# A graph layer on one core: each gather of source rows takes 127 rows instead of 128

## The chip, the cores and the metric

The kernel runs on one core of one Trainium2 chip. The core has a matrix engine (PE), a vector engine (DVE), an activation engine (ACT), GpSimd (POOL) and a queue engine for transfers (SP); sixteen DMA engines move data between the core's memory (SBUF) and the device's (DRAM). The metric is the device time of one execution in microseconds (us), and lower is better. The change is judged by the median of several executions.

## The reference: what is computed

A graph has 12,500 nodes with 96 numbers each and 412,500 edges, sorted by the node that they point to (`dst`). Per edge, a message is made from the row of its source node, the row of its target node and four numbers of its own; the messages are normalized over all edges, summed by target, and added to a term of the node itself.

```python
node_feat = _mlp(x, W_node, b_node, g_node, beta_node)
edge_feat = _mlp(edge_attr, W_edge, b_edge, g_edge, beta_edge)
row, col = (edge_index[0], edge_index[1])
message = jnp.concatenate([x[row], x[col], edge_feat], axis=1)
message = _mlp(message, W_msg, b_msg, g_msg, beta_msg)
agg = jax.ops.segment_sum(message, col, num_segments=node_feat.shape[0])
return agg + node_feat
...
x = _layernorm(x + _L0_gnn_ref(...))
```

`_mlp` is `relu(h @ W + b)`, normalized by mean and variance over all rows. So the sums of the messages and of their squares over all 412,500 edges are needed, as well as the sums by target.

## The kernel before

**Tables.** Since the message's matrix acts on three concatenated parts, the part of the source is done once per node: `p_tab` holds x times the first 96 rows of the matrix, `q_tab` x times the second 96. Per edge, a row of `p_tab` is fetched by its source, and what `q_tab` and the edge's own numbers give is added.

**Edges in blocks.** A *tile* is 128 edges, one on each partition. Four tiles are a group (`GT`), four groups of 512 edges are a block (`BG`, 16 tiles, 2048 edges). The sorted edges are laid out so that a tile takes 32 edges from each of the block's four groups: partitions 0 to 31 from the first, 96 to 127 from the fourth. There are 3223 tiles, 806 groups and 202 blocks, the last of them with seven tiles.

**The gather (L205 to L218).** POOL fetches the source rows: one indirect transfer per tile, with 128 row numbers from one column of `src`, writes 128 rows of 384 bytes to `pg`, one on each partition. 3220 tiles are fetched so (64 of them from x itself for the first four blocks, whose product with the matrix is done later, 3156 from `p_tab`); the last tile of three groups (`EARLY`) is fetched row by row by SP. The tile `pg` holds two groups, and seven such tiles are a ring of 14 groups. Each gather signals one of eight counters in turn, and waits for the gather eight before it, which used the same one.

**Ahead of the main loop.** From the start POOL gathers the rows of 29 blocks, which SP stores to DRAM as they come (`spill`, L237), and after them fills the ring with 14 groups. Meanwhile the tables are made, the edges' numbers are split into parts of bf16 and stored as `stack_d`, the node term is computed, and `edge_norm` (L394) computes the statistics of the edge features: per block three matmuls (L413), a relu on ACT (L417) and three statistics on DVE (L419), on tiles `eas` that DVE sets to ones first (L401).

**The main loop (L731 to L767)** walks over the blocks in an order fixed by `plan`: from block 29 on, with the 29 stored blocks strewn in between (they are read back as `pb`, and so need no gather then). Each step `k` is one group. For the block two steps of blocks ahead PE makes the edge features and the window of places (L605/L614) and ACT applies relu (L621, 127 partitions: 96 features, 31 window places; `rhs` holds the matching rows, which SP loads per block from 31 rows of `q_tab` at L578). For the next block PE makes `z` (L626) and DVE transposes it in 32x32 squares so that edges stand on partitions (L636). For the present group pair `message` (L649) adds the gathered rows to `z` and cuts at zero, on DVE. ACT squares the message (L663), DVE adds the squares up (L674). DVE writes a 0/1 matrix of the edges' targets within the block's window (L655), PE multiplies the messages by it (L693), and DVE adds the sums to `agg` (L712, L713). At the end of a step `ahead_of` puts one more group of gathers on POOL (L763): the first group of a pair may only overwrite its `pg` when `message` has read it.

The instructions of PE, DVE, ACT, POOL and SP in the main loop stand in the order in which the code is written (`manual_schedule`); elsewhere a scheduler orders PE, DVE and ACT.

**The end (L770 to L798)** handles the last, incomplete block of two groups: POOL folds the squares (`collect`, L682 and L684), PE adds the sums over partitions, and then the output is normalized and written (from L975 on).

Of the kernel before, what the change touches and what calls it, by code (L numbers as in the profile page):

```python
# [13 lines left out]
F32 = mybir.dt.float32  # L14
# [3 lines left out]
AF = mybir.ActivationFunctionType  # L18
OP = mybir.AluOpType
AX = mybir.AxisListType  # L20
# [4 lines left out]
N, C, E, ED = 12500, 96, 412500, 4  # L25
EPS = 1e-5
P = 128
# [13 lines left out]
RW = 7  # L41
NBQ = RW * 32
# [27 lines left out]
NW = WS * (BG - 1) + WN + 1  # L70
QE = 32
BT = BG * GT
LT = NT - (NBL - 1) * BT
LE, LS = LT * QE, 7
CL, CE = 3, 1
# [35 lines left out]
def gnn(ctx, tc, t):  # L111
# [93 lines left out]
    def gather(g, pg, without=0):  # L205
        c, o = g * GT // CW, g * GT % CW
        tab, idx = (t["x"], src_raw[:, g * GT:]) if g < RAW * BG else (p_tab, src[:, c % 2, o:])
        if c and o == CW // 2 and (c + 1) * CW < NTP:
            sources(c + 1)
        made = [nc.gpsimd.indirect_dma_start(  # L210
            out=pg[:, i, :], out_offset=None, in_=tab[:, :],
            in_offset=bass.IndirectOffsetOnAxis(ap=idx[:, i:i + 1], axis=0)).ins
            for i in range(min(GT, NT - g * GT) - without)]
        for x in made[:-1]:
            tc.add_to_no_dep_group(f"rows{g}", x)
        if made[:-1]:
            tc.declare_fence(made[-1], group=f"rows{g}")
        return pg  # L218

    def blocks():  # L220

        waiting = []
        for b in range(SPILL // BG + BEHIND):
            if b < SPILL // BG:
                for i in range(0, BG, 2):
                    pg = ring.tile([P, 2, GT, C], F32, name="pg")
# [167 lines left out]
    def edge_norm():  # L394

        with tc.tile_pool(name="es", bufs=2) as work, tc.tile_pool(name="es1", bufs=1) as one, \
# [3 lines left out]
            for x in eas:  # L400
                nc.vector.memset(x[C:], 1.0)  # L401
            for b in range(NBL):
                if b % J == 0:
                    yield
                    ea, n = eas[b // J % 2], min(J, NBL - b)
                    stacked(ea[:, :n, :], b, n)
                    if b + n == NBL:
                        nc.sync.dma_start(ea[ON:, n - 1, :], t["one"])
                for i in range(NS):
                    k = NS * b + i  # L410
                    if k % 2 == 0:
                        pr = ps.tile([P, 2, GE], F32, name="pr")
                    nc.tensor.matmul(pr[:, k % 2, :], wide[:, P * i:P * (i + 1)], ea[:, b % J, :],  # L413
                                     start=True, stop=True)
                    if k % 2:
                        r = work.tile([P, 2, GE], F32, name="r", bufs=4)
                        nc.scalar.activation(r, pr, AF.Relu)  # L417
                        for o in (1, 0):
                            nc.vector.bn_stats(stats[:, (k - o) % NS, (k - o) // NS, :], r[:, 1 - o, :])  # L419
# [66 lines left out]
    def fast(ring):  # L486
        y0s, got = [], {}

        def ahead_of(g):
            if g % 2 == 0:  # L490
                got[g] = ring.tile([P, 2, GT, C], F32, name="pg")
            if g < NG:
                gather(g, got[g // 2 * 2][:, g % 2, :, :])
# [27 lines left out]
        with tc.tile_pool(name="fix", bufs=1) as fix, tc.tile_pool(name="msg", bufs=2) as work, \  # L521
# [117 lines left out]
            def message(k, m=2, n=2 * GT):  # L639

                s, g = steps[k]
                o = k % 2 * GT
                z = zs[s % 2][:, g % BG * GT:g % BG * GT + n, :]
                h = hb[k // 2 % HP].rearrange("p m t c -> p (m t) c")[:, o:o + n, :C]
                if order[s] < RAW:
                    nc.vector.tensor_scalar(h, z, 0.0, MOST, op0=OP.max, op1=OP.min)
                    return
                rows = got[g // 2 * 2].rearrange("p m t c -> p (m t) c")[:, o:o + n, :]
                nc.vector._custom_dve(TENSOR_ADD_SAT, out=h, in0=z, in1=rows, s0=MOST, s1=0.0)  # L649
# [11 lines left out]
            def squared(k, m=2, n=GT):  # L661
                sq = work.tile([P, 2, GT, C], F32, name="sq")
                nc.scalar.activation(sq[:, :m, :n, :], hb[k // 2 % HP][:, k % 2:k % 2 + m, :n, :C], AF.Square)  # L663
                return sq

            def valid(t):

                left_over = E - (NBL - 1) * BT * P - (BG - 1) * LE
                return P - QE + min(max(left_over - (t - (NBL - 1) * BT) * QE, 0), QE) if t >= (NBL - 1) * BT else P

            def moments(sq, at_last):

                sq = sq.rearrange("p m t c -> p (m t) c")
                nc.vector.tensor_tensor(wide_sq, wide_sq, sq, op=OP.add)  # L674
                if at_last:
                    nc.vector.tensor_reduce(squares, wide_sq.rearrange("p t c -> p c t"), axis=AX.X, op=OP.add)

            def collect(x, n):
                plus = nc.gpsimd.tensor_add
                while n > 1:  # L680
                    half = n // 2
                    plus(x[:, :half * C], x[:, :half * C], x[:, (n - half) * C:n * C])  # L682
                    n -= half
                plus(squares, x[:, :C], squares)  # L684

# [32 lines left out]
            with tc.manual_schedule(engines={ET.SP, ET.Pool, ET.PE, ET.DVE, ET.Activation}):  # L718
# [12 lines left out]
                for k in range(last):  # L731
# [24 lines left out]
                    if s + 2 < len(order):  # L756
# [13 lines left out]
                s, g = len(order) - 1, steps[last][1]  # L770
                m = NT - (g + 1) * GT
# [7 lines left out]
                sq.append(work.tile([P, 2, GT, C], F32, name="sq"))  # L779
                nc.vector.memset(sq[1][:, 0, :, :], 0.0)  # L780
                h = hb[(n - 1) // 2 % HP]
                for t in range(m):
                    r = valid((g + 1) * GT + t)
                    nc.scalar.activation(sq[1][:r, 0, t, :], h[:r, 1, t, :C], AF.Square)
                collect(sq[0][:, 0, :, :].rearrange("p t c -> p (t c)"), GT)
                sums(last)
                at_end = place(s - 1), place(s)
                unread(1)
                collect(sq[1][:, 0, :, :].rearrange("p t c -> p (t c)"), m)
                add(s - 1, at_end[0])  # L790
                sums(n - 1)
                unread(1)
                square_sum = by_place[s % 2][:C, P:P + 1]
                nc.tensor.matmul(square_sum, squares, ones, start=True, stop=True)
                unread(BUSY)
# [11 lines left out]
    def general():  # L807

        with tc.tile_pool(name="gd", bufs=1, space=DRAM) as gd, tc.tile_pool(name="gfix", bufs=1) as fix, \
# [111 lines left out]
            with tc.For_i(0, NI, 1) as it:  # L921
# [3 lines left out]
                for g in range(-AHEAD, IG):  # L925
                    if g + AHEAD < IG:
                        got[g + AHEAD] = gather(si, di, (g + AHEAD) * GT, GT, P)
                    if g < 0:
# [3 lines left out]
                    nc.vector.memset(ea, 1.0)  # L932
                    nc.sync.dma_start(ea[:ED], t["ea"][i::BG, bass.ds(it * (IG // BG) + g // BG, 1), :]
                                      .rearrange("k b e -> k (b e)"))
# [6 lines left out]
            for j, (t0, nt, rows) in enumerate(REST):  # L941
# [6 lines left out]
                nc.vector.memset(ea, 1.0)  # L948
                of = t["ea"][i::BG, g // BG, o:o + nt * rows] if g < BG * (NBL - 1) else t["ea_end"][i::BG, o:o + nt * rows]
                nc.sync.dma_start(ea[:ED, :nt * rows], of)  # L950
                message(j, got, ea[:, :nt * rows], df, sp, c, nt, rows, stats[:, NI * IG + j, :])
# [135 lines left out]
```

## Time and profile before

| what | value |
|---|---|
| median of 3 runs (lowest to highest) | 4238.63 us (4232.95 to 4239.72) |
| the profiled execution: time, span of its trace | 4239.95 us, 4238.2 us |
| gathers from `p_tab` on POOL | 3156, median 947 ns |
| first and last start of them | 83.6 and 4175.2 us |
| DVE's wait for a gather at L649 | 583.0 us, 172 times |
| DMA engines' mean share in the main loop | 0.24 |

How to read it: a profile of one execution gives the busy time of each engine, groups of instructions by line with their count, busy time and mean duration, and for the idle time ahead of an instruction what ended it ("<-DMA pg" is a transfer into pg that landed, "<-issue" is that nothing the profile shows was waited for). In a tile's view the three durations are the least, the median and the greatest in ns. DMA views give packets, megabytes and rates; their rows of 40 digits or numbers are 40 equal slices of a stretch, the digits in tenths of the sixteen engines' time.

### The profile page before, as it was taken

To read this page: it belongs to the slowest core of one execution; us is meant where nothing else is said; L and a number is where in the kernel's file an instruction comes from. 1 tells how busy PE (TensorE), PEld (TensorE's weight loads), DVE (VectorE), ACT (ScalarE), POOL (GpSimd) and SP (SyncE) were. 2 spreads that over 40 slices of the span, in tenths; PEclk is the share of its full clock that TensorE was granted. 3 is DMA by queue.
4 is the path that set the end of the run, shared out by engine and by line. 5 is a ranking of instruction groups with operands and counts; after the bars stand their busy time and mean duration, and the time that the engine had idled before them with its cause. 6 is when DMAs were issued, how large, how long until landed. Compare 5 with 4: busy or idle time off the path is not lost.

```text
span 4238.2 us, 34504 instructions
## 1 busy us (share of the span) xinstructions
PE 2500.7 (59%) x10245; PEld 1391.0 (33%) x10245; DVE 3340.1 (79%) x4652; ACT 1117.9 (26%) x1229; POOL 3180.5 (75%) x3248
## 2 busy tenths in 40 slices
PE   4156664776655655666655565555655556666556
PEld 3041111433333332333333333333333333333335
DVE  2469998998887877878878887787878877878775
ACT  1438882222221211212112211111112112211111
POOL 7777776777777777777777777777777777777775
PEclk7557776888877787877777877787788787777776
DMA  8746562222222223222222222222222222222222
GB/s 229 267 139 149 134 148 51 57 57 64 50 56 53 57 71 78 63 56 56 55 56 50 57 54 55 57 57 54 56 57 53 50 63 50 54 57 55 56 44 64
DMA packets 215122, 316.63 MB, mean 75 GB/s; under 512 B 126785, under 2 KB 133275, under 8 KB 212095
## 3 DMA queue, kind: packets, MB, share of 16 engines
q0 software_dynamic: 103040, 158.48, 17.6%
q1 hardware_dynamic: 98923, 150.92, 12.1%
q10 hardware_dynamic: 12960, 4.93, 0.5%
q8 instruction: 82, 1.34, 0.1%
q14 instruction: 117, 0.96, 0.1%
HBM read 258.19 MB, written 55.89 MB: 74 GB/s over the span
## 4 chain that ended last, share of the span: by engine, by line
POOL 37%; DVE 25%; issue 19%; DMA 12%; PE 6%; ACT 1%; SPq 0%; DVEq 0%; POOLq 0%; ACTq 0%
POOL pg L210 37%; DMA pg<-p_tab,src 9%; DVE big L636 9%; DVE estats L419 8%; DVE h L649 3%; DVE mixed L674 2%; PE z L626 1%; PE pa L693 1%; PE py L981 1%; DVE at L655 1%; DMA q_tab<-trow 1%; PE py L383 1%; PE pt L194 0%; DMA x<-in_ea 0%; DVE part L424 0%
## 5 line engine op out<-in xcount | busy, mean ns | idle before, releaser
L210 POOL DMA_INDIRECT pg<-p_tab,src x3156 | 3097.6, 981 | 995.2 <-issue 899.6
L636 DVE STREAM_TRANSPOSE big<-z 32x512 f32<-32x512 f32 x2424 | 1715.3, 708 | 90.8 <-PE z L626 29.6
L693 PE MATMUL pa<-at,h 128*97 128x80 f32 x6446 | 934.1, 304 | 1346.3 <-DVE h L649 1327.5
L693 PEld LDWEIGHTS pa<-at,h 128*97 128x97 f32 x6446 | 881.7, 217 | 1818.7 <-DVE h L649 1677.1
L626 PE MATMUL z<-left,rhs 128*96 128x512 f32 (+1 forms) x1616 | 1079.7, 757 | 2.1 <-DVE big L636 2.1
L663 ACT ACTIVATE sq<-h 128x768 f32<-128x768 f32 x403 | 339.5, 842 | 2750.2 <-DVE h L649 2710.1
L649 DVE CUSTOM_DVE_ANT_0 h<-big,pg 128x768 f32<-128x768 f32 x346 | 325.3, 940 | 585.1 <-DMA pg<-p_tab,src 583.0
L621 ACT ACTIVATE left<-pr 127x1024 f32<-127x1024 f32 x404 | 405.6, 1004 | 18.1 <-PE pr L614 18.1
L674 DVE TENSOR_TENSOR mixed<-mixed,sq 128x768 f32<-128x768 f32 x401 | 387.7, 967 | 12.5
L419 DVE BATCH_NORM_STATS2 estats<-r 128x6 f32<-128x512 f32 x606 | 359.7, 682 | 11.8 <-ACT r L417 11.8
L417 ACT ACTIVATE r<-pr 128x1024 f32<-128x1024 f32 x303 | 309.0, 1025 | 102.2 <-PE pr L413 54.4
L413 PE MATMUL pr<-ea,wide 128*128 128x512 bf16 x606 | 237.8, 486 | 126.8 <-ACT r L417 116.7
L655 DVE TENSOR_TENSOR at<-rel,mixed 128x1264 f32<-128x1264 bf16 x202 | 296.5, 1468 | 6.8
L614 PE MATMUL pr<-late,we 128*128 128x512 bf16 x692 | 287.1, 507 | 23.4 <-DMA rhs<-q_tab 12.2
L626 PEld LDWEIGHTS z<-left,rhs 128*96 128x96 f32 x1616 | 264.1, 212 | 8.0 <-DVE big L636 6.5
L614 PEld LDWEIGHTS <-we 128*128 128x128 bf16 x808 | 103.3, 128 | 448.2 <-issue 446.5
L413 PEld LDWEIGHTS <-wide 128*128 128x128 bf16 x606 | 66.6, 110 | 297.4 <-issue 277.9
L383 PE MATMUL py<-center,big 96*128 96x96 f32 x196 | 42.8, 423 | 113.2 <-ACT big L378 100.2
L383 PEld LDWEIGHTS py<-center,big 96*128 96x128 f32 x196 | 42.0, 332 | 114.0 <-ACT big L378 100.6
L210 POOL DMA_INDIRECT pg<-in_x,src_raw x64 | 61.0, 952 | 20.9 <-issue 19.2
L194 PE MATMUL pt<-w_msg,big 96*128 96x192 f32 x196 | 37.8, 360 | 19.6 <-ACT trow L198 13.4
L200 DVE COPY trow<-pt 128x768 f32<-128x768 f32 x14 | 13.1, 956 | 44.5 <-DMA p_tab<-trow 20.7
(128 smaller groups left out, 696.6 us busy)
## 6 DMA issues: line engine op xcount, KB each, us to landing
pg<-p_tab,src POOLq DMA_INDIRECT x3156
pb<-spill SPq DMA_DIRECT2D x29, 768.0 KB
spill<-pg SPq DMA_DIRECT2D x55, 384.0 KB
ea<-stack_d SPq DMA_DIRECT2D x25, 480.0 KB
stack_d<-y SPq DMA_DIRECT2D x24, 448.0 KB
late<-stack_d SPq DMA_DIRECT2D x57, 180.0 KB
rhs<-q_tab SPq DMA_DIRECT2D x202, 46.5 KB
x<-in_ea SPq DMA_DIRECT2D x8, 896.0 KB
```

The costliest lines, as they stand in the source:

```text
L210: made = [nc.gpsimd.indirect_dma_start(out=pg[:, i, :], out_offset=None, in_=tab[:, :], in_offset=bass.IndirectOffsetOnAxis(ap=idx[:, i:i ...
L417: nc.scalar.activation(r, pr, AF.Relu)
L419: nc.vector.bn_stats(stats[:, (k - o) % NS, (k - o) // NS, :], r[:, 1 - o, :])
L614: nc.tensor.matmul(prs[s, half][:, i, :n], we[:, 2 * half + i, :], block[s][:, :n], start=True, stop=True)
L621: nc.scalar.activation(x[:C + WN, 2 * half:2 * half + 2, :n], pr[:C + WN, :, :n], AF.Relu)
L626: nc.tensor.matmul(zt[i % ZB][:C, :n], rhs[:KR, s % RB, i, :], left[s % 2][:KR, i, :n], start=True, stop=not raw)
L636: nc.vector.transpose(zs[s % 2][i * QE:(i + 1) * QE, :n // QE, q * QE:(q + 1) * QE], zt[i % ZB][q * QE:(q + 1) * QE, :n].rearrange("p (t e ...
L649: nc.vector._custom_dve(TENSOR_ADD_SAT, out=h, in0=z, in1=rows, s0=MOST, s1=0.0)
L655: nc.vector.tensor_tensor(at[s % AB][:, :m, :NW - 1], rel.rearrange("p g t -> p (g t)")[:, order[s] * BT:order[s] * BT + m].unsqueeze(2) . ...
L663: nc.scalar.activation(sq[:, :m, :n, :], hb[k // 2 % HP][:, k % 2:k % 2 + m, :n, :C], AF.Square)
L674: nc.vector.tensor_tensor(wide_sq, wide_sq, sq, op=OP.add)
L693: nc.tensor.matmul(by_place[s % 2][:C + 1, :NW], hb[k // 2 % HP][:r, k % 2, t, :], at[s % AB][:r, i * GT + t, :], start=i == 0 and t == 0, ...
```

## The change

The partition 127 of every gathered tile is left empty. A gather names 127 rows and writes 127 partitions. A tile now takes 32 edges from the first three groups of a block and 31 from the fourth, so that a full block holds 16 x 127 = 2032 edges. The edges fill 203 full blocks, and the last block has one tile: 204 blocks, 3249 tiles. What follows from it:

- `message`, the squares, their sums and the matmuls of L693 use 127 partitions.
- The ring is seven fixed tiles instead of a pool of seven buffers; DVE sets their partitions 96 to 127 to zero at the start, as partition 127 is never gathered but is stored and transposed with the rest.
- As a fixed tile may only be overwritten in program order after its reader, `ahead_of` is called twice at each second step, instead of once at each step.
- In `edge_norm` the rows of ones are no longer written by DVE, but loaded by SP: the empty places of a full block must be zero there, and the ones' row now carries the valid places.
- The last block's handling shrinks to one tile.
- The arrays that the host lays out follow the new places.

```diff
 GT, GE, BG = 4, 512, 4
-NT = -(-E // P)
+QE = 32
+BT = BG * GT
+PT = P - 1
+EB = BT * PT
+NBL = -(-E // EB)
+LT = -(-(E - (NBL - 1) * EB) // QE)
+LE, LS = LT * QE, 0
+LR = E - (NBL - 1) * EB
+assert LT == 1
+NT = (NBL - 1) * BT + LT
 NG = -(-NT // GT)
-NBL = -(-NG // BG)
...
-    ring = rpool.enter_context(tc.tile_pool(name="ring", bufs=RING // 2))
+    ring = rpool.enter_context(tc.tile_pool(name="ring", bufs=1))
+    ring = [ring.tile([P, 2, GT, C], F32, name=f"pg{i}") for i in range(RING // 2)]
+    for x in ring:
+        nc.vector.memset(x[C:], 0.0)
...
-            out=pg[:, i, :], out_offset=None, in_=tab[:, :],
-            in_offset=bass.IndirectOffsetOnAxis(ap=idx[:, i:i + 1], axis=0)).ins
+            out=pg[:PT, i, :], out_offset=None, in_=tab[:, :],
+            in_offset=bass.IndirectOffsetOnAxis(ap=idx[:PT, i:i + 1], axis=0)).ins
...
             for x in eas:
-                nc.vector.memset(x[C:], 1.0)
+                nc.sync.dma_start(x[ON:], t["one"][:, 0:1, :].to_broadcast([P - ON, J, GE]))
...
-                z = zs[s % 2][:, g % BG * GT:g % BG * GT + n, :]
-                h = hb[k // 2 % HP].rearrange("p m t c -> p (m t) c")[:, o:o + n, :C]
+                z = zs[s % 2][:PT, g % BG * GT:g % BG * GT + n, :]
+                h = hb[k // 2 % HP].rearrange("p m t c -> p (m t) c")[:PT, o:o + n, :C]
...
-                rows = got[g // 2 * 2].rearrange("p m t c -> p (m t) c")[:, o:o + n, :]
+                rows = got[g // 2 * 2].rearrange("p m t c -> p (m t) c")[:PT, o:o + n, :]
...
-                return P - QE + min(max(left_over - (t - (NBL - 1) * BT) * QE, 0), QE) if t >= (NBL - 1) * BT else P
+                return PT if t < (NBL - 1) * BT else LR
...
-                nc.vector.tensor_tensor(wide_sq, wide_sq, sq, op=OP.add)
+                nc.vector.tensor_tensor(to, to, sq, op=OP.add)
...
-                    if g >= SPILL and ahead < SPILL + len(steps):
-                        ahead_of(ahead)
-                        ahead += 1
+                    if g >= SPILL and u % 2:
+                        for _ in range(2):
+                            ahead_of(ahead)
+                            ahead += 1
...
-                message(last, 1, GT)
-                sq = [squared(last, 1, GT)]
+                message(last, 1, LT)
+                sq = work.tile([P, 2, GT, C], F32, name="sq")
+                nc.vector.memset(sq[:, 0, 0, :], 0.0)
+                nc.scalar.activation(sq[:LR, 0, 0, :], hb[last // 2 % HP][:LR, 0, 0, :C], AF.Square)
                 sums(last - 2)
                 sums(last - 1)
                 unread(BUSY - 1)
-                message(n - 1, 1, m)
...
-                collect(sq[0][:, 0, :, :].rearrange("p t c -> p (t c)"), GT)
+                collect(sq[:, 0, 0, :], 1)
...
+        out[:-1, :BG - 1] = full[:, :n].reshape((NBL - 1, BG - 1, BT, QE) + a.shape[1:])
+        out[:-1, BG - 1, :, :QE - 1] = full[:, n:].reshape((NBL - 1, BT, QE - 1) + a.shape[1:])
```

How the order on POOL moves is seen at two places. The first is where the main loop begins: these are the last gather ahead of it, the load of a flag, the first eight gathers of the main loop and the first of the next eight. Before (DMASW4 and the like are the eight counters, and the wait is for the gather eight before; `DVE` is `message` having read the buffer; `pg_4908` and so on are buffers of the pool):

```order
L210 DMA pg_4908<-p_tab_64,src_72 128x96 [waits DMASW4_49]
L719 TENSOR_LOAD flag_114 [waits DVE_49]
L210 DMA pg_5049<-p_tab_64,src_72 128x96 [waits DMASW5_49,DVE_49]
L210 DMA pg_5049<-p_tab_64,src_72 128x96 [waits DMASW6_49]
L210 DMA pg_5049<-p_tab_64,src_72 128x96 [waits DMASW7_49]
L210 DMA pg_5049<-p_tab_64,src_72 128x96 [waits DMASW0_49]
L210 DMA pg_5049<-p_tab_64,src_72 128x96 [waits DMASW1_49]
L210 DMA pg_5049<-p_tab_64,src_72 128x96 [waits DMASW2_49]
L210 DMA pg_5049<-p_tab_64,src_72 128x96 [waits DMASW3_49]
L210 DMA pg_5049<-p_tab_64,src_72 128x96 [waits DMASW4_49]
L210 DMA pg_5077<-p_tab_64,src_72 128x96 [waits DMASW5_49,DVE_49]
```

Each row is one gather of 128 rows of 96 numbers, and only the first of eight waits for DVE. Now, at the same place (`pg1` to `pg3` are tiles of the fixed ring):

```order
L217 DMA pg1_78<-p_tab_64,src_72 127x96 [waits DMASW4_49]
L725 TENSOR_LOAD flag_128 [waits DVE_49]
L217 DMA pg2_79<-p_tab_64,src_72 127x96 [waits DMASW5_49,DVE_49]
L217 DMA pg2_79<-p_tab_64,src_72 127x96 [waits DMASW6_49]
L217 DMA pg2_79<-p_tab_64,src_72 127x96 [waits DMASW7_49]
L217 DMA pg2_79<-p_tab_64,src_72 127x96 [waits DMASW0_49]
L217 DMA pg2_79<-p_tab_64,src_72 127x96 [waits DMASW1_49]
L217 DMA pg2_79<-p_tab_64,src_72 127x96 [waits DMASW2_49]
L217 DMA pg2_79<-p_tab_64,src_72 127x96 [waits DMASW3_49]
L217 DMA pg2_79<-p_tab_64,src_72 127x96 [waits DMASW4_49]
L217 DMA pg3_80<-p_tab_64,src_72 127x96 [waits DMASW5_49,DVE_49]
```

The waits are the same and stand at the same gathers, and the number of gathers ahead of the flag is the same; only the shape differs. The second place is the whole of POOL's gathers and its end. Before (`sq` and `squares` are the squares' sums, `xN` counts equal rows):

```order
L210 DMA pg<-in_x,src_raw 128x96 x64
L210 DMA pg<-p_tab,src 128x96 x453
L719 TENSOR_LOAD flag
L210 DMA pg<-p_tab,src 128x96 x2703
L682 TENSOR_TENSOR sq<-sq 128x384
L682 TENSOR_TENSOR sq<-sq 128x192
L682 TENSOR_TENSOR sq<-sq 128x96
L684 TENSOR_TENSOR squares<-sq,squares 128x96
L682 TENSOR_TENSOR sq<-sq 128x192
L682 TENSOR_TENSOR sq<-sq 128x96
L684 TENSOR_TENSOR squares<-sq,squares 128x96
L682 TENSOR_TENSOR sq<-sq 128x96 x2
```

Now, the last gather (the 3246th, the one tile of the last block) and what follows it:

```order
L217 DMA pg_77<-p_tab,src 127x96
L688 TENSOR_TENSOR sq<-sq 127x384
L688 TENSOR_TENSOR sq<-sq 127x192
L688 TENSOR_TENSOR sq<-sq 127x96
L690 TENSOR_TENSOR squares<-sq,squares 127x96 x2
```

The main loop's part grows from 2703 to 2729 gathers, and five instructions follow the last of them instead of ten.

More of the change, by code (lines that the diff above doesn't have):

```diff
@@ L225, in blocks @@
                 for i in range(0, BG, 2):
-                    pg = ring.tile([P, 2, GT, C], F32, name="pg")
+                    pg = ring[(b * BG + i) // 2 % len(ring)]
                     for k in range(2):
@@ L407, in edge_norm @@
                     if b + n == NBL:
-                        nc.sync.dma_start(ea[ON:, n - 1, :], t["one"])
+                        nc.sync.dma_start(ea[ON:, n - 1, :], t["one"][:, 1, :])
                 for i in range(NS):
@@ L490, in ahead_of @@
             if g % 2 == 0:
-                got[g] = ring.tile([P, 2, GT, C], F32, name="pg")
+                got[g] = ring[g // 2 % len(ring)]
             if g < NG:
@@ L777, in fast @@
                 unread(BUSY - 1)
-                message(n - 1, 1, m)
[L779 to L784, printed above, removed]
-                collect(sq[0][:, 0, :, :].rearrange("p t c -> p (t c)"), GT)
-                sums(last)
[L787 to L792, printed above, removed]
+                collect(sq[:, 0, 0, :], 1)
+                at_end = place(s - 1), place(s)
+                add(s - 1, at_end[0])
+                sums(last)
+                unread(2)
                 square_sum = by_place[s % 2][:C, P:P + 1]
-                nc.tensor.matmul(square_sum, squares, ones, start=True, stop=True)
+                nc.tensor.matmul(square_sum, squares[:PT], ones[:PT], start=True, stop=True)
                 unread(BUSY)
@@ L1012, with slots @@
     s, d = np.asarray(inputs["src"]), np.asarray(inputs["dst"])
-    d = np.pad(d, (0, EP - E), mode="edge")
-    whole = (NBL - 1) * GE * BG
+    whole = (NBL - 1) * EB
+    def slots(a, fill=None):
+        out = np.zeros((NBL, BG, BT, QE) + a.shape[1:], a.dtype)
+        full = a[:whole].reshape((NBL - 1, EB) + a.shape[1:])
+        n = (BG - 1) * GE
+        out[:-1, :BG - 1] = full[:, :n].reshape((NBL - 1, BG - 1, BT, QE) + a.shape[1:])
+        out[:-1, BG - 1, :, :QE - 1] = full[:, n:].reshape((NBL - 1, BT, QE - 1) + a.shape[1:])
+        if fill is not None:
+            out[:-1, BG - 1, :, QE - 1] = out[:-1, BG - 1, :, QE - 2]
+            out[-1] = a[-1]
+        out[-1, 0, 0, :LR] = a[whole:]
+        return out
     def tiles(a):
-        end = a[whole:whole + LE * BG].reshape(BG, LT, QE).transpose(0, 2, 1).reshape(P, LT)
-        a = a[:whole].reshape(NBL - 1, BG, BT, QE).transpose(1, 3, 0, 2).reshape(P, -1)
-        return np.pad(np.concatenate([a, end], axis=1), ((0, 0), (0, BT - LT)))
+        return a.transpose(1, 3, 0, 2).reshape(P, NTP)
     def groups(a):
-        out = np.zeros((NBQ, BG, GE) + a.shape[1:], a.dtype)
-        out[:NBL - 1] = a[:whole].reshape((NBL - 1, BG, GE) + a.shape[1:])
-        out[NBL - 1, :, :LE] = a[whole:whole + LE * BG].reshape((BG, LE) + a.shape[1:])
-        return out
-    s = np.pad(s, (0, EP - E))
-    give("src", tiles(s))
-    give("src_all", s.reshape(NTP, P).T)
-    give("lasts", tiles(s).T[GT - 1::GT])
-    give("dst", tiles(d))
-    give("dst_all", d.reshape(NTP, P).T)
-    base = d[::GE * BG]
+        a = a.reshape((NBL, BG, GE) + a.shape[4:])
+        return np.pad(a, [(0, NBQ - NBL)] + [(0, 0)] * (a.ndim - 1))
+    give("src", tiles(slots(s)))
+    give("src_all", np.pad(s, (0, NTP * P - E)).reshape(NTP, P).T)
+    give("lasts", tiles(slots(s)).T[GT - 1::GT])
+    give("dst", tiles(slots(d, True)))
+    give("dst_all", np.pad(d, (0, NTP * P - E)).reshape(NTP, P).T)
+    base = d[::EB]
     give("base", base.reshape(1, NBL))
@@ L1039 @@
     give("later", later.reshape(P, RW))
-    give("dlin", groups(d).transpose(1, 0, 2).reshape(P, RW, GE))
+    give("dlin", groups(slots(d, True)).transpose(1, 0, 2).reshape(P, RW, GE))
     first = np.repeat(np.arange(BG), QE)
@@ L1045 @@
     ea = np.asarray(inputs["edge_attr_4"])
-    ea = np.pad(ea, ((0, EP - E), (0, 0)))
-    give("ea", groups(ea).transpose(3, 1, 0, 2).reshape(ED * BG, NBQ, GE))
-    give("ea_end", ea[whole:].reshape(BG, GE, ED).transpose(2, 0, 1).reshape(ED * BG, GE))
+    give("ea", groups(slots(ea)).transpose(3, 1, 0, 2).reshape(ED * BG, NBQ, GE))
+    ea = np.pad(ea, ((0, NBL * BG * GE - E), (0, 0))).reshape(NBL, BG, GE, ED)
+    give("ea_all", ea.transpose(3, 1, 0, 2).reshape(ED * BG, NBL, GE))
     for name in ("x", "L0_gnn_W_node", "L0_gnn_W_msg"):
@@ L1073 @@
     give("wp", wp.astype(ml_dtypes.bfloat16))
-    left = np.clip(E - whole - np.arange(BG) * LE, 0, LE)
-    give("one", np.tile(np.arange(GE)[None, :] < left[:, None], (5, 1)).astype(ml_dtypes.bfloat16))
+    valid = slots(np.ones(E, np.float32)).reshape(NBL, BG, GE)[[0, -1]]
+    give("one", np.tile(valid.transpose(1, 0, 2), (5, 1, 1)).astype(ml_dtypes.bfloat16))
     give("L0_gnn_b_msg", np.asarray(inputs["L0_gnn_b_msg"]).reshape(1, C))
```

23 lines of the change are left out of this document (8 added, 15 removed).

## The prediction

> **What bounds the kernel now.** I read the page's busy shares first, then the chain of work that ended last, then the gathers' own rows.
>
> ```profile
> PE 2500.7 (59%) x10245; PEld 1391.0 (33%) x10245; DVE 3340.1 (79%) x4652; ACT 1117.9 (26%) x1229; POOL 3180.5 (75%) x3248
> POOL 37%; DVE 25%; issue 19%; DMA 12%; PE 6%; ACT 1%; SPq 0%; DVEq 0%; POOLq 0%; ACTq 0%
> ```
>
> By busy time DVE leads with 79%, but the chain runs through POOL (37%) and "issue" (19%), time in which an engine waited for nothing that is shown. The answer on the tile pg and the rows of the main loop (700 us to the last gather) say whose time that is; a group's row has busy time, mean ns of one, and the idle time ahead of it with what ended it.
>
> ```profile
> L210 POOL DMA_INDIRECT pg<-p_tab,src x3156: 941/947/4143, 83.6 to 4175.2; - x198
>   issue: 918.8, 3013
> ...
> L210 POOL DMA_INDIRECT pg<-p_tab,src x2703 | 2641.8, 977 | 842.0 <-issue 767.1 <-DMA pg<-p_tab,src 41.2 <-DVE h L649 18.1
> DVE h L649 <- DMA pg<-p_tab,src: 579.8, 171, 8.1
> 700.00:4177.00 3477.00, 2098.47 (x8958) 1186.52 (x8958) 2791.46 (x3828) 711.80 (x811) 2642.64 (x2704) 0.79 0.24 56
> ```
>
> POOL issues gathers back to back from 83.6 to 4175.2 us: 947 ns each by the median, and after almost every one 918.8 / 3013 = 305 ns of idle time for which the profile names no cause. In the main loop 2703 gathers take 2641.8 + 842.0 = 3483.8 us; without the one wait of 18.1 us that is 3465.7 / 2703 = 1.282 us each, and the stretch is only 3477 us long. So POOL's gathers are the main loop. DVE is the consumer: 171 times it waits at L649 for the newest gather, 579.8 us together. POOL is the bound, DVE follows with 579.8 us to spare, and a transfer's own length doesn't count, as 14 groups are fetched ahead.
>
> **Part 1: more gathers.** A full block has 16 x 127 = 2032 edges instead of 2048, so 412,500 edges need 203 full blocks and one tile: 203 x 16 + 1 = 3249 tiles, less three fetched row by row, 3246 gathers against 3156 + 64 = 3220. The 517 gathers ahead of the main loop stay (the order's rows have 64 + 453 ahead of the flag), so all 26 are in the main loop, 2729 there. At 1.282 us each: **+33.3 us**. DVE gets two more blocks' work, 2791.46 / 201 = 13.9 us each by the window's row (201 whole blocks), 28 us, hidden in its 579.8 us of waiting.
>
> **Part 2: what a gather of 127 rows costs POOL.** This is the disputed term: the trace holds no gather of another size. Two kinds of rows are near. The first tells how a transfer is spread: the page's queue row, and eight microseconds of the DMA view in slices of 0.2 us, in which one window load `rhs` (31 partitions x 4 x 384 B) runs among the gathers.
>
> ```profile
> q0 software_dynamic: 103040, 158.48, 17.6%
> ...
> DMA  0910000830000551000390000082000094000045
> GB/s 0 200 31 15 4 0 0 171 98 16 12 19 21 111 144 48 12 19 21 65 200 16 0 0 0 0 200 46 0 0 0 0 169 77 0 0 0 0 108 138
> ...
> q0 software_dynamic: 216, 0.34, 20.1%
> q1 hardware_dynamic: 125, 0.05, 2.1%
> ...
> rhs<-q_tab SPq DMA_DIRECT2D x1, 46.5 KB
> ```
>
> 103,040 / 3220 = 32 packets a gather and 158.48 MB / 3220 = 49.2 KB, that is 128 x 384 B and 64 B more: as I read it, 16 engines with one packet of 8 rows and one small write each. The bursts agree: about 0.4 us at near 200 GB/s each 1.25 us. The load of 31 partitions is another thing: 125 packets are its 124 rows and one write, and they trickle at 12 to 21 GB/s between the bursts, some 3 us for 46.5 KB: one engine. 31 and 127 are both prime, so I take it that a gather of 127 rows goes to one engine too. The second kind of row is what the issuing queue pays for the one and the other (min/median/max, ns):
>
> ```profile
> L578 SPq DMA_DIRECT2D rhs<-q_tab x202: 228/257/2800, 687.5 to 4106.7; - x101
> L360 SPq DMA_DIRECT2D late<-stack_d x174: 318/427/3002, 676.4 to 4067.6; - x174
> ```
>
> `late` loads 16, 32 or 60 partitions. The one-engine load is issued 318 - 228 = 90 ns (least) to 427 - 257 = 170 ns (median) faster. That is SP's hardware queue, not POOL's software, but it is the nearest row, and POOL too has to serve one engine's queue with rows instead of sixteen. POOL's unexplained 305 ns would fit sixteen such steps of 19 ns. I take the middle, 130 ns a gather, nearer to neither end because neither row is POOL's. The ends: above, all of the 305 ns but what lies between two ordinary POOL instructions; the next row has 0.2 us ahead of four, 50 ns, so up to 255 ns. Below, 947/128 = 7 ns if the price goes by rows, nothing if it goes by instruction; and less than nothing if writing 127 rows into one queue is slower work, which no row excludes.
>
> ```profile
> L682 POOL TENSOR_TENSOR sq<-sq 128x96 f32<-128x96 f32 x4 | 1.8, 440 | 0.2
> ```
>
> 2729 x 130 ns = **-354.8 us** (90 ns: -245.6; 170 ns: -463.9). POOL's main loop is then 2729 x 1.152 = 3144 us. DVE's floor is 3477 - 579.8 + 28 = 2925 us, so POOL stays the bound, with DVE's waits down to about 220 us.
>
> [...]
>
> **Part 3: a gather in flight longer.** Each gather waits for the one eight before it (the DMASW names in the order's rows). At 1.152 us that is 9.2 us of room. One engine needs some 3 us for 46.5 KB instead of the burst's 0.4, so the main loop has room. The first 700 us are different; the second view of the page has the DMA engines at four to eight tenths there:
>
> ```profile
> DMA  8746562222222223222222222222222222222222
> ```
>
> At six tenths, 3 us become 3 / 0.4 = 7.5 us, close to the room. I cost it at nothing: in that part POOL would gain 517 x 0.13 = 67 us and had 18.1 us of waiting for DVE at its end. Without that cover it costs what the excess is.
>
> The moved call of the gathers (two groups at every second step instead of one at each) costs nothing: in both orders the first gather of a pair carries the wait for DVE's message and the seven behind it do not, so POOL stands in front of the same wait. The index load that a gather puts on SP moves with it by one step, and has a second buffer. Instructions on 127 partitions instead of 128 cost the same: of two relu groups of ACT the one on 127 isn't dearer.
>
> ```profile
> L621 ACT ACTIVATE left<-pr 127x1024 f32<-127x1024 f32 x404 | 405.6, 1004 | 18.1 <-PE pr L614 18.1
> L417 ACT ACTIVATE r<-pr 128x1024 f32<-128x1024 f32 x303 | 309.0, 1025 | 102.2 <-PE pr L413 54.4
> ```
>
> **Part 4: ahead of the main loop.** DVE's chain sets this part, as the 18.1 us show. Two memsets go to the DMA queue (-6.9 us) and two blocks give six more statistics (6 x 0.682 = +4.1):
>
> ```profile
> L419 DVE BATCH_NORM_STATS2 estats<-r 128x6 f32<-128x512 f32 x606 | 359.7, 682 | 11.8 <-ACT r L417 11.8
> L401 DVE MEMSET ea<- 32x4096 bf16 x2 | 6.9, 3472 | 1.8 <-issue 1.8
> ```
>
> **-2.8 us**. The two loads put on SP in their place stand ahead of the first `ea` load; at the 0.43 us of the `late` row they add 0.9 us there at most, and I leave them out. The seven memsets of the ring stand first on DVE, while POOL waits for its indices; each gather needs only its own tile's. I cost them at nothing (about 1 us if the first is late).
>
> **Part 5: the end.** The chain after the last gather:
>
> ```profile
> 4175.19 0.95 POOL pg L210
> 4176.15 1.01 POOL sq L682
> ...
> 4181.35 0.39 POOL squares L684
> 4181.78 0.48 PE pa L794 x2
> ```
>
> 5.6 us of POOL sums ran there; five of ten instructions go. But the last gather now lands some 2.6 us later and its one tile's message stands behind it. **-1 us**.
>
> **The sum.** The profiled execution took 4239.95 us, its span 4238.2; the median of the runs is 4238.63, 1.3 lower, which I neglect. 4240 + 33.3 - 354.8 - 2.8 - 1 = 3914.7: **3915 us**, with 3806 to 4024 by the two SP rows.
>
> **The rivals.** *The price is the instruction's* (slower). POOL spends 947 + 305 ns whatever the engines, or the change doesn't do what it says and the generator spreads 127 rows over sixteen engines as before. Then 4240 + 33.3 - 3.8 = 4269.5, or 4250 if 7 ns go with the row. It decides below 29.5 / 2729 = 11 ns of saving. For it: all 3156 gathers have the same 947 ns, so the trace holds no proof that the count of engines is in it. Against it: SP's rows. [...]
>
> *DVE becomes the bound.* From 1.282 - 2925 / 2729 = 0.21 us of saving the rest is lost: 4240 - 579.8 + 28 - 3.8 = 3684 us, with a few waits left near 3700. For it: up to 255 ns lie in the idle time alone. Against it: SP's rows stop at 170.
>
> *One engine is too slow* (slower). If a gather's landing exceeds 10.3 us, eight in flight no longer fill 1.282 us: at 12 us it is 1.5 us a gather, 2729 x 0.218 = 595 us, 4860 us; and if all gathers got the same engine, 3 us each, near 9700 us. For it: 127 random rows are harder than the 124 of the load, and other packets share the engine. Against it: 3 us of 10.3.
>
> **How the numbers follow.** Forecast 0.50, price of the instruction 0.26, DVE's floor 0.14, one engine too slow or the generator dearer 0.10. 0.2% (8.5 us) is about what a measurement of this kernel can tell from no change. Of the 0.26, 0.06 falls within it (a saving of 8 to 14 ns), and 0.01 of the forecast: faster 0.63, same 0.07, slower 0.30. The range takes in DVE's floor and the unchanged price, 3690 to 4275; above it stands the 0.10 of slow engines. The forecast's own range is 3800 to 4110.
>
> **What would show it.** Right: a median of L210 below 947 or an idle time below 305 ns, together about 130 less; DVE's wait at L649 near 220 us; main loop near 3150 us; the software queue's packets about one engine's worth a gather, with the bursts gone from the DMA view. Wrong: 947 and 305 unchanged and the main loop 33 us longer; DVE without waits (the floor); or POOL waiting for DMA pg, now 41.2 us, for hundreds.

## The result, and the profile after

The changed kernel takes 9376.05 us (median of 4 runs, 9369.52 to 9382.79) where the kernel before takes 4238.47: 2.2127 times as long (95% interval 2.2089 to 2.2165). The forecast was 3915 us, in a range of 3690 to 4275.

The page of the changed kernel, its busy shares and the shares of the chain:

```profile
PE 2736.2 (29%) x10179; PEld 1582.0 (17%) x10327; DVE 3383.8 (36%) x4700; ACT 1108.2 (12%) x1237; POOL 8346.1 (89%) x3269
POOL 81%; issue 13%; DMA 4%; DVE 1%; PE 1%; SPq 0%; ACT 0%; DVEq 0%; POOLq 0%; ACTq 0%
```

DVE's busy time hardly moved (3340.1 to 3383.8 us), ACT's neither, and POOL's grew from 3180.5 to 8346.1. The chain is POOL, 81%, with "issue" behind it. The gathers' rows in the tile view of POOL and the groups by line say why:

```profile
L217 POOL DMA_INDIRECT pg<-p_tab,src x3182: 2544/2549/3841, 194.5 to 9317.2; - x199
L217 POOL DMA_INDIRECT pg<-in_x,src_raw x64: 2544/2549/5588, 4.2 to 191.7; - x64
its engine sat idle before it (us, times) until:
  issue: 983.6, 3227
  DVE pg L136: 2.7, 1
  DMA ea<-stack_d: 1.8, 6
...
DMA to landing us min/median/max: 6.1/7.1/18.5
...
L217 POOL DMA_INDIRECT pg<-p_tab,src x3182 | 8155.6, 2563 | 969.9 <-issue 965.0
...
L217 POOL DMA_INDIRECT pg<-in_x,src_raw x64 | 170.8, 2669 | 21.9 <-issue 18.6
```

A gather that names one row fewer takes POOL 2549 ns instead of 947, from the first to the last, and the least (2544) and the median lie close together. The idle time behind it is what it was, 983.6 / 3227 = 305 ns. The two groups add up to 8155.6 + 969.9 + 170.8 + 21.9 = 9318 us of a span of 9381 us: the kernel is its gathers, end to end. DVE now waits for a gather ahead of every message: 341 messages in 7818 us of the main loop, 341 waits, where before it was 171 waits for 345 messages (the second row counts the messages).

```profile
DVE h L656 <- DMA pg<-p_tab,src: 4920.1, 341, 16.7
...
L656 DVE CUSTOM_DVE_ANT_0 h<-big,pg x341: 957/958/961, 1499.1 to 9298.1; 127x768 f32<-127x768 f32 x171
```

What was moved is told by the queue's row (packets, MB, share) and by eight microseconds of the DMA view in slices of 0.2 us:

```profile
q0 software_dynamic: 675168, 183.24, 19.8%
...
DMA  3232222100000244133111100000361412212000
GB/s 7 24 26 5 4 26 46 2 21 21 21 21 21 45 39 5 4 27 46 5 3 24 43 21 21 21 12 2 26 6 3 48 4 26 25 24 63 21 21 0
...
pg<-p_tab,src POOLq DMA_INDIRECT x4, 7.1
```

The bursts near 200 GB/s are gone; in many slices the data trickles at 21 to 26 GB/s, not far from the 12 to 21 of the load of 31 partitions. That looks like one engine: from 5001.6 to 5002.6 us, five such slices of 21 GB/s, the DMA share is 0.07 of the sixteen engines, 1.1 of them. But 675,168 / 3246 = 208 packets a gather, 13 for each of sixteen engines on average, where it was 2 (103,040 / 3220 = 32 packets); and 183.24 MB / 3246 = 56,451 bytes. The 127 rows are 48,768 of them, 64 are what the prediction found beyond the rows in a gather of 128 as well (158.48 MB / 3220 = 49,217 bytes, 65 more than 128 x 384, to within 2 by the rounding of the MB), and what is left, 7,619, is 15 x 127 x 4 = 7,620. So my estimate from these totals and the share is that the rows do go to one engine, and that the fifteen engines without rows get a filler of 4 bytes for each row that the one engine gets. No view shows a filler by itself; the experiments give three more totals that fit. A gather lands 7.1 us after its issue by the median, 6.1 at the least: POOL is done with it long before it lands.

### The profile page after: what moved, and what is told of

The parts are those of the page before. It is cut to its first block, busy times and chain, and to the rows that moved or that the text cites. A ratio compares the mean times of both kernels' runs of the same rounds, so it can differ in the third digit from the quotient of the medians.

```text
span 9381.1 us, 34644 instructions
## 1 busy us (share of the span) xinstructions
PE 2736.2 (29%) x10179; PEld 1582.0 (17%) x10327; DVE 3383.8 (36%) x4700; ACT 1108.2 (12%) x1237; POOL 8346.1 (89%) x3269
## 3 DMA queue, kind: packets, MB, share of 16 engines
q0 software_dynamic: 675168, 183.24, 19.8%
## 4 chain that ended last, share of the span: by engine, by line
POOL 81%; issue 13%; DMA 4%; DVE 1%; PE 1%; SPq 0%; ACT 0%; DVEq 0%; POOLq 0%; ACTq 0%
POOL pg L217 81%; DMA pg<-p_tab,src 1%; DMA ea<-stack_d 1%; DMA p_tab<-trow 1%; DVE big L643 0%; DMA q_tab<-trow 0%; PE py L978 0%; SPq L468 0%; DVE mixed L680 0%; DMA basei<-in_base 0%; DMA whole<-in_wq 0%; DMA spill<-pg 0%; DMA ea<-in_one 0%; DMA x<-in_ea 0%; DVE at L662 0%
## 5 line engine op out<-in xcount | busy, mean ns | idle before, releaser
L217 POOL DMA_INDIRECT pg<-p_tab,src x3182 | 8155.6, 2563 | 969.9 <-issue 965.0
L699 PE MATMUL pa<-at,h 127*97 127x80 f32 x6498 | 1076.5, 334 | 5515.4 <-DVE h L656 5478.6
L656 DVE CUSTOM_DVE_ANT_0 h<-big,pg 127x768 f32<-127x768 f32 (+1 forms) x349 | 333.6, 956 | 5006.4 <-DMA pg<-p_tab,src 5006.4
L699 PEld LDWEIGHTS pa<-at,h 127*97 127x97 f32 x6498 | 1026.2, 247 | 5999.4 <-DVE h L656 5837.5
L633 PE MATMUL z<-left,rhs 128*96 128x512 f32 x1632 | 1205.8, 831 | 3.2 <-DVE big L643 3.2
L670 ACT ACTIVATE sq<-h 127x768 f32<-127x768 f32 x406 | 342.2, 843 | 7225.6 <-DVE h L656 7186.2
L628 ACT ACTIVATE left<-pr 127x1024 f32<-127x1024 f32 (+1 forms) x408 | 409.0, 1003 | 76.6 <-PE pr L621 76.6
L680 DVE TENSOR_TENSOR mixed<-mixed,sq 127x768 f32<-127x768 f32 x405 | 391.3, 966 | 12.7
L621 PE MATMUL pr<-late,we 128*128 128x512 bf16 (+1 forms) x584 | 282.3, 561 | 76.6 <-DMA late<-stack_d 70.7
L217 POOL DMA_INDIRECT pg<-in_x,src_raw x64 | 170.8, 2669 | 21.9 <-issue 18.6
```

What stands on the lines that cost most here:

```text
L217: made = [nc.gpsimd.indirect_dma_start(out=pg[:PT, i, :], out_offset=None, in_=tab[:, :], in_offset=bass.IndirectOffsetOnAxis(ap=idx[:PT, ...
L621: nc.tensor.matmul(prs[s, half][:, i, :n], we[:, 2 * half + i, :], block[s][:, :n], start=True, stop=True)
L628: nc.scalar.activation(x[:C + WN, 2 * half:2 * half + 2, :n], pr[:C + WN, :, :n], AF.Relu)
L633: nc.tensor.matmul(zt[i % ZB][:C, :n], rhs[:KR, s % RB, i, :], left[s % 2][:KR, i, :n], start=True, stop=not raw)
L670: nc.scalar.activation(sq[:PT, :m, :n, :], hb[k // 2 % HP][:PT, k % 2:k % 2 + m, :n, :C], AF.Square)
L680: nc.vector.tensor_tensor(to, to, sq, op=OP.add)
```

## The experiments

**The gathers back at 128 rows, the rest of the change kept.**

```diff
-            out=pg[:PT, i, :], out_offset=None, in_=tab[:, :],
-            in_offset=bass.IndirectOffsetOnAxis(ap=idx[:PT, i:i + 1], axis=0)).ins
+            out=pg[:, i, :], out_offset=None, in_=tab[:, :],
+            in_offset=bass.IndirectOffsetOnAxis(ap=idx[:, i:i + 1], axis=0)).ins
```

> The changed kernel with its gathers back at 128 rows, all else of the change kept (partition 127 gets a row that nothing uses). Theory A, the generator walks one step per row of the fullest engine's share, so that 127 rows on one engine cost 127 steps where 128 rows on sixteen cost 8: the gather is back at a median of 947 ns, and what is left is 26 more gathers at 1.28 us less some 4 us ahead and behind, 4270 us (4255 to 4285). Theory B, the rest of the change costs it too (the fixed ring, the moved calls, work on 127 partitions): clearly above 4300 us, with idle time of POOL ahead of L217 that isn't the 305 ns.

Measured: 4274.93 us, where the kernel before took 4244.05 on that chip, ratio 1.0068 (1.0055 to 1.0081). The gathers' tile view and the main loop's group:

```profile
L217 POOL DMA_INDIRECT pg<-p_tab,src x3182: 940/944/3160, 84.0 to 4209.6; - x199
...
L217 POOL DMA_INDIRECT pg<-p_tab,src x2729 | 2672.3, 979 | 854.6 <-issue 750.3 <-DMA pg<-p_tab,src 64.0 <-DVE h L656 23.2
```

The 5100 us are gone with the one row, and what stays is 30.9 us. 2729 gathers take 2672.3 + 854.6 - 23.2 = 3503.7 us, 1.284 us each, as the 2703 of before took 1.282. Theory A holds here, and the rest of the change costs its 26 gathers and nothing else that shows.

**Ten counts of rows in one kernel.** The gathers of the main loop name another count each 68 groups. The kernel was run once; what is read is POOL's time for each count, not its total.

```diff
+SIZES = [(128, C), (126, C), (125, C), (124, C), (120, C), (118, C), (113, C), (112, C), (32, C), (127, C)]
...
-        nc.vector.memset(x[C:], 0.0)
+        nc.vector.memset(x, 0.0)
...
+        r, w = SIZES[min((g - SPILL) // 68, len(SIZES) - 1)] if g >= SPILL else (P, C)
...
-            out=pg[:PT, i, :], out_offset=None, in_=tab[:, :],
-            in_offset=bass.IndirectOffsetOnAxis(ap=idx[:PT, i:i + 1], axis=0)).ins
+            out=pg[:r, i, :w], out_offset=None, in_=tab[:, :w],
+            in_offset=bass.IndirectOffsetOnAxis(ap=idx[:r, i:i + 1], axis=0)).ins
```

> The changed kernel, whose gathers in the main loop name 128, 126, 125, 124, 120, 118, 113, 112, 32 and 127 rows in turn, 68 groups (272 gathers) each; rows that aren't fetched stay zero or old, so part of the messages is left out. Theory A: with k the largest divisor of the count up to 16 and n rows on each of k engines, a gather takes 839 + 13.46 n ns (a line through 947 ns at n = 8 and 2549 ns at n = 127): 128 gives 947, 126 (14 x 9) 960, 125 (5 x 25) 1176, 124 (4 x 31) 1256, 120 (15 x 8) 947, 118 (2 x 59) 1633, 113 (1 x 113) 2360, 112 (16 x 7) 933, 32 (16 x 2) 866, 127 2549. Theory B, any count that is no multiple of 16 is written row by row: 126, 125, 124, 120, 118, 113 all between 2300 and 2550. Theory C, POOL waits for the engine that moves the rows: few rows per engine cost no more than 947, and 118 and 113 go with bytes.

Measured, in ten stretches of the trace, one for each count (least/median/greatest ns, first and last start); in order of time 128, 126, 125, 124, 120, 118, 113, 112, 32 and 127 rows:

```profile
L219 POOL DMA_INDIRECT pg<-p_tab,src x260: 942/947/2296, 619.9 to 979.3; - x130
L219 POOL DMA_INDIRECT pg<-p_tab,src x264: 968/986/2351, 994.1 to 1344.6; - x132
L219 POOL DMA_INDIRECT pg<-p_tab,src x268: 1182/1199/1874, 1354.0 to 1759.8; - x134
L219 POOL DMA_INDIRECT pg<-p_tab,src x265: 1278/1283/2592, 1769.0 to 2193.5; - x133
L219 POOL DMA_INDIRECT pg<-p_tab,src x267: 979/981/2307, 2204.0 to 2559.7; - x134
L219 POOL DMA_INDIRECT pg<-p_tab,src x266: 1628/1633/1742, 2568.9 to 3083.2; - x133
L219 POOL DMA_INDIRECT pg<-p_tab,src x267: 2350/2355/3713, 3099.0 to 3808.4; - x134
L219 POOL DMA_INDIRECT pg<-p_tab,src x266: 922/927/2232, 3821.5 to 4158.4; - x133
L219 POOL DMA_INDIRECT pg<-p_tab,src x268: 860/865/1922, 4167.3 to 4499.9; - x134
L219 POOL DMA_INDIRECT pg<-p_tab,src x334: 2537/2542/3705, 4509.1 to 5462.7; - x167
```

| rows | engines x rows each, by theory A | theory A, ns | measured median, ns |
|---|---|---|---|
| 128 | 16 x 8 | 947 | 947 |
| 126 | 14 x 9 | 960 | 986 |
| 125 | 5 x 25 | 1176 | 1199 |
| 124 | 4 x 31 | 1256 | 1283 |
| 120 | 15 x 8 | 947 | 981 |
| 118 | 2 x 59 | 1633 | 1633 |
| 113 | 1 x 113 | 2360 | 2355 |
| 112 | 16 x 7 | 933 | 927 |
| 32 | 16 x 2 | 866 | 865 |
| 127 | 1 x 127 | 2549 | 2542 |

The line was drawn through two points and meets the others within 34 ns, over a range of 1677. The division into engines is theory A's; no view names the engines of a gather. Theory B falls with 126, 125, 124 and 120, far below 2300. Theory C named 947 ns for few rows on each engine and didn't say whether 25 and 31 are few, so the next experiment has to decide it. Where theory A counts 1, 2 or 16 engines the line is met within 7 ns in this table; where it counts 4, 5, 14 or 15 the gather takes 23 to 34 ns more, for which I have no cause.

**Narrow and wide rows.** As above, with other counts, and with rows of 24 numbers instead of 96; again one run.

```diff
+SIZES = [(128, C), (128, 24), (127, C), (127, 24), (122, C), (119, C), (64, C), (16, C), (15, C), (113, 24)]
...
-            out=pg[:PT, i, :], out_offset=None, in_=tab[:, :],
+            out=pg[:r, i, :w], out_offset=None, in_=(tab if w == C else tab.rearrange("n (a c) -> (n a) c", c=w))[:, :],
```

> The changed kernel, whose gathers in the main loop name in turn 128 rows of 96 numbers, 128 of 24, 127 of 96, 127 of 24, 122 of 96, 119 of 96, 64 of 96, 16 of 96, 15 of 96 and 113 of 24, 272 gathers each (rows of 24 numbers come from another place of the table, so messages are wrong or left out there). Theory A, POOL's own steps: the width doesn't matter, 127 rows of 24 numbers take 2549 ns as those of 96 do, 113 of 24 take 2360; 122 (2 x 61) 1660, 119 (7 x 17) 1068, 64 (16 x 4) 893, 16 and 15 (one row an engine) 852. Theory C, POOL waits for the engine that moves the rows: 127 rows of 24 numbers, a quarter of the bytes, fall clearly below 2549, towards 950.

Measured, in order of time: 128 rows of 24 numbers, 127 of 96, 127 of 24, 122 of 96 and 16 of 96:

```profile
L219 POOL DMA_INDIRECT pg<-p_tab,src x265: 943/947/2166, 994.8 to 1336.8; - x133
L219 POOL DMA_INDIRECT pg<-p_tab,src x268: 2537/2542/3650, 1344.6 to 2109.3; - x134
L219 POOL DMA_INDIRECT pg<-p_tab,src x268: 2537/2542/3720, 2123.5 to 2908.9; - x134
...
L219 POOL DMA_INDIRECT pg<-p_tab,src x267: 1655/1660/3022, 2924.2 to 3448.9; - x134
...
L219 POOL DMA_INDIRECT pg<-p_tab,src x266: 835/840/1807, 4195.3 to 4524.0; - x133
```

A quarter of the bytes changes nothing, 2542 ns both times, and 947 as before with 128 rows. So POOL didn't wait for the bytes to move here. The other counts took 1092 ns (119), 902 (64), 871 (15) and 2359 (113 narrow), against 1068, 893, 852 and 2360 by the line; 16 rows took 840 against 852.

POOL could still wait for an engine that needs a fixed time for each row, wide or narrow. The places in the kernel of ten counts where one count follows another speak against it (start, duration, idle time ahead; first from 32 to 127 rows, then from 113 to 112):

```profile
4502.22 0.87 POOL L219 DMA_INDIRECT pg<-p_tab,src  x1 [0.30 <-issue]
4503.39 2.55 POOL L219 DMA_INDIRECT pg<-p_tab,src  x1 [0.30 <-issue]
...
3816.39 2.36 POOL L219 DMA_INDIRECT pg<-p_tab,src  x1 [0.30 <-issue]
3819.05 0.93 POOL L219 DMA_INDIRECT pg<-p_tab,src  x1 [0.30 <-issue]
```

The first gather of 127 rows comes straight after gathers of 32 rows and takes 2.55 us at once; the first of 112 comes straight after gathers of 113 and takes 0.93 us at once. The duration went by the gather itself and not by what was issued before it: theory C falls. What POOL does in that time, no run tells.

The two kernels test the fillers too. By an estimate with theory A's division, 64 bytes a gather and a filler of 4 bytes for each row that an engine falls short of the fullest, they move 149.56 and 102.53 MB; without fillers it would be 143.54 and 95.02. The queue's rows, first of the ten counts, then of the narrow and wide rows:

```profile
q0 software_dynamic: 245872, 149.58, 16.1%
...
q0 software_dynamic: 197344, 102.44, 20.8%
```

**One row fewer again.**

```diff
-            out=pg[:PT, i, :], out_offset=None, in_=tab[:, :],
-            in_offset=bass.IndirectOffsetOnAxis(ap=idx[:PT, i:i + 1], axis=0)).ins
+            out=pg[:PT - 1, i, :], out_offset=None, in_=tab[:, :],
+            in_offset=bass.IndirectOffsetOnAxis(ap=idx[:PT - 1, i:i + 1], axis=0)).ins
```

> The changed kernel with gathers of 126 rows, one fewer again (one row of each tile stays zero, so one message in 127 lacks its source). Theory A: 126 rows are 14 engines with 9 rows, 839 + 9 x 13.46 = 960 ns, so the whole kernel is back near 4270 + 3246 x 0.013 = 4312 us at the most, faster than with 127 rows by more than half. Theory B, counts that are no multiple of 16 are written row by row: about 2535 ns a gather and 9300 us.

Measured: 4457.37 us, ratio 1.0518 (1.0500 to 1.0535) to the kernel before, and less than half of the kernel with 127 rows. The tile view, the main loop's group and the queue:

```profile
L217 POOL DMA_INDIRECT pg<-p_tab,src x3182: 995/999/2597, 91.4 to 4406.7; - x199
...
L217 POOL DMA_INDIRECT pg<-p_tab,src x2733 | 2872.2, 1051 | 836.7 <-issue 767.5 <-DMA pg<-p_tab,src 62.5 <-DVE h L656 4.4
...
q0 software_dynamic: 103872, 157.50, 14.6%
```

Theory A is right in kind and B falls; the ceiling of 4312 us is passed by 145. A gather took 999 ns and not 960, and its mean stands 52 ns over the median where that of 128 rows stands 35 over (979 to 944); (2872.2 + 836.7 - 4.4) / 2733 = 1.356 us each, 72 ns over those of 128 rows, times 2729 is 196 us, of which 182 are seen. Why 126 rows took 999 here and 986 in the kernel of ten counts stays open, and so does why the mean stands further above the median. The queue agrees with the fillers: 157.50 MB / 3246 = 48,521 bytes, 126 x 384 + 2 x 9 x 4 + 64 = 48,520, by theory A's division two idle engines with nine fillers each.

**Two versions of the kernel before.** The profile of before and that of the first experiment showed POOL waiting for DVE at the start of the main loop, 18.1 and 23.2 us. If gathers are the bound, more of them before that point are worth their time.

```diff
-SPILL = 29 * BG
+SPILL = 30 * BG
```

> The kernel before with 30 blocks stored ahead of the main loop instead of 29, so that POOL gathers during the 18.1 us in which it waited for DVE at the main loop's start. If POOL's gathers are the only bound of the main loop, 16 gathers move out of it (20.5 us) into 18.1 us of idle time and a little more: 4220 us, 18 us (0.4%) below the kernel before. If the stored block costs DVE or the transfers more than that, no change or slower.

Measured: 4226.6 us against 4245.65, ratio 0.9958 (0.9944 to 0.9972), 19 us. POOL's wait for `message` is no longer among its longest; this is the fastest kernel of the study.

```diff
-RING = 14
+RING = 16
```

> The kernel before with a ring of 16 groups instead of 14, so that POOL has 8 more gathers to issue in the same 18.1 us. If POOL's gathers are the only bound, 8 x 1.28 = 10 us less: 4228 us, 0.25% below. If the 18.1 us are not idle time that ends up in the total, no change.

Measured: 4234.94 us against 4245.65, ratio 0.9975 (0.9964 to 0.9986), 10.7 us. The size is right, the place isn't: of POOL's waits, first of the kernel before,

```profile
POOL pg L210 <- DMA spill<-pg: 18.7, 13, 4.3
POOL pg L210 <- DVE h L649: 18.1, 1, 18.1
```

and then of the one with the larger ring,

```profile
POOL pg L210 <- DVE h L649: 19.2, 1, 19.2
POOL pg L210 <- DMA spill<-pg: 4.2, 5, 2.2
```

the 18.1 us stayed, and the waits for stores that have to leave a ring tile before it is filled again fell from 18.7 to 4.2 us.

## Why the prediction was wrong

**What bounds the kernel: right.** POOL's gathers are the loop. The kernels with 127, 128 and 126 rows differ by their gathers' price times their count, and the two last ones gained what gathers moved or hurried are worth.

**Part 1, 26 more gathers at 1.282 us: right.** The first experiment has this part together with parts 4 and 5, without part 2. The parts' sum was +33.3 - 2.8 - 1 = 29.5 us; measured were 30.9, and by the ratio's interval 23 to 34.

**Part 2, the step that failed.** The forecast took 130 ns off a gather, "nearer to neither end because neither row is POOL's", from SP's loads with one engine and with many. The gather became 1602 ns dearer. Against the first experiment, which differs only in the rows named, that is 5101 us for the kernel, where the forecast had -354.8. It is more than the main loop's share, as the 517 gathers ahead of it got dearer too: the first message starts at 1374.6 us instead of 709.3.

The first half of the reading fits what was measured: the 56,451 bytes of a gather are those of 127 rows on one engine with the estimated fillers, and the DMA share was 0.07, 1.1 of sixteen engines, while 21 GB/s moved. That this would follow from 127 being prime was the author's estimate, from the one load of 31 partitions.

The second half, that serving one engine is less work, is false for POOL: no run shows a saving with one engine, and what the runs showed in its place is 2549 ns instead of 947. Its time went with the rows that theory A puts on the fullest engine: 839 ns and 13.46 ns for each such row, 8 of them with 128 rows and 127 with 127, come within 39 ns of every median of a gather in the experiments. The bytes moved fit the estimate of fillers that give every engine as many entries as the fullest. What POOL does for each such row no view shows. The two SP rows couldn't have told it: they are another queue, and besides the engines their loads differ in shape and size.

The idle 305 ns, which "would fit sixteen such steps of 19 ns", stayed with 127 rows as with 128 (983.6 / 3227 and 918.8 / 3013), and are not explained by this.

The lower bound was where this could have been caught. Its words "less than nothing if writing 127 rows into one queue is slower work, which no row excludes" name what happened, and then give it no price; the sum and the range have no term for it. The price could be bounded from the row: 947 ns for 8 rows on each engine (the prediction's reading of 32 packets a gather), if all of it were in the rows, is 118 ns a row and 15 us for 127. With an end so far out, 0.10 was too little.

**Part 3: not put to the test.** The landing takes 7.1 us from the issue, 2.5 of them POOL's own time, where 3 us were reckoned with for the transfer; but at 2.85 us a gather, eight in flight leave 22.8 us, and POOL waited for no gather.

**Part 4, -2.8 us: right in size.** The first gather of the main loop, in the kernel before and then in the first experiment (start, duration, and idle time ahead of it):

```profile
691.44 0.94 POOL L210 DMA_INDIRECT pg<-p_tab,src  x1 [0.30 <-issue]
710.50 0.95 POOL L210 DMA_INDIRECT pg<-p_tab,src  x1 [18.12 <-DVE h L649]
```

```profile
682.67 0.94 POOL L217 DMA_INDIRECT pg<-p_tab,src  x1 [0.30 <-issue]
706.86 0.94 POOL L217 DMA_INDIRECT pg<-p_tab,src  x1 [23.25 <-DVE h L656]
```

It starts 3.6 us earlier, by one profile of each; the two items of the sum were not measured apart. **Part 5, -1 us:** from the last gather's start to the end of the span are 4238.2 - 4175.2 = 63.0 us before and 4272.4 - 4209.6 = 62.8 in the first experiment, 0.2 us less; a difference that small decides nothing.

**The rivals.** *The price is the instruction's* gives the time of the kernel with 128 rows named: 30.9 us above the kernel before, against 29.5. For 127 rows it is false. *DVE becomes the bound* went the other way, as DVE waited for 4920.1 us. *One engine is too slow* had the right sign and the wrong place: it was priced as eight gathers in flight waiting for one engine, while POOL waited for no transfer and a quarter of the bytes cost the same. That its far end, "near 9700 us", lies close to the measured 9376 is luck: it came from 3 us of transfer for each gather, and what costs 2.85 us is POOL's issuing.

## What to carry to other kernels

A price read from one issuing path didn't hold for another: SP's hardware queue issued the load of 31 partitions 90 to 170 ns faster than `late` (228 and 257 ns, least and median, against 318 and 427), and going from 128 rows to 127 made POOL's gather 1602 ns slower. Where an instruction is the bound and its size is to change, its price at the new size is worth one kernel that runs it at ten sizes, before a layout is built for it; ten prices here took one run. For gathers like these, take a count that sixteen divides: 16, 32, 64, 112 and 128 rows took 840, 865, 902, 927 and 947 ns, one row off a full tile multiplied the gather's time by 2.7 (2549 ns), and 120 and 126 rows, with 981 and 986 to 999 ns, cost more than 128.

## What the runs showed of the hardware that was not expected

- An indirect gather took POOL 840 ns with 16 rows, 871 with 15, 865 with 32, 944 to 947 with 128, 1633 with 118 and 2542 to 2549 with 127, and the same with 24 numbers a row as with 96 (947 with 128 rows, 2542 with 127). The rows on the fullest engine, as theory A divides them, give these and all other medians to within 39 ns; that division is an estimate.
- A gather of 127 rows moved 7,619 bytes more than its rows and the 64 bytes beyond them. By my estimate these are fillers of four bytes for each step on engines without rows, 7,620 bytes: the bytes moved by the kernels of 126 and of 127 rows and by the two of many counts fit this within 0.1%.
- The idle time behind a gather that the profile gives no cause for was 305 ns in the mean with 128 rows and with 127, and 304 to 305 ns at each count and width of the two kernels of ten sizes (72.2 / 237 with 32 rows, 102.1 / 335 with 113 of 24 numbers).
